# Attention scores in 17 stretches with one half-filled PSUM bank each, in place of 16 full ones

## The chip, the core and the metric

The kernel runs on one core of a Trainium2 chip. The metric is the device time of one execution in microseconds (us); lower is better. TensorE is called PE in the profile, its weight loads PEld; VectorE is DVE, ScalarE is ACT, GpSimd is POOL, SyncE is SP.

## The reference, cut to what matters

Three residual blocks follow each other on x of 4 x 1024 x 512, each closed by a layer normalisation: an attention, a gated convolution over two taps, and a ternary feed-forward. The change touches the attention alone:

```python
q = _lin(_lin(x, wq_w, wq_b), vq_w, vq_b)      # k and v in the same way
q = q.reshape(b, s, hc, H).transpose(2, 0, 1, 3)   # 32 heads (hc) of 16 columns (H)
scores = jnp.einsum('cbqh,cbkh->cbqk', q, k) / scale
attn = jax.nn.softmax(scores, axis=-1)
o = jnp.einsum('cbqk,cbkh->cbqh', attn, v)
o = o.reshape(H, b, s, hc).transpose(1, 2, 0, 3).reshape(b, s, f)
return _lin(o, wo_w, wo_b)
```

So there are 4 batches with 32 heads each, 1024 queries and 1024 keys, and a head has 16 columns.

## The kernel before

**Units.** The attention is cut into 32 units. A unit is four heads of one batch. Each of the four heads sits in its own group of 32 partitions (two halves, high and low, of 16 columns), so that its score products use 32 rows of TensorE's array and the four heads use four different row groups.

**Two passes over the scores.** Every score is computed twice. `nat(u, ...)` (L696, product at L712) makes scores with queries on the partitions, 128 queries by 512 keys in one PSUM bank, from two products of 512 columns. DVE takes each row's largest (`mx`, L725, written negated). When half of a unit is done, two keys' halves are joined (`least`, L730), POOL splits the result in a high and a low part (`neg`, L734), and `shift` (L741) turns it (L745) and sends it through DRAM into the rows `m_rows`. `scores(u, ...)` (L761, product at L791) then makes the scores with keys on the partitions, 128 keys by 256 queries, from three products of 256 columns: two for the halves of q and k, one that adds the negated maximum (`ones` times `m_rows`). Two such blocks fill one PSUM bank. ACT takes the exponential of the whole bank into an `at` tile (L800).

**V products.** `weigh(u, i)` (L818, products at L828) multiplies the exponentials with V for 256 queries and half of the keys: 16 products, 32 instructions, on 128 rows and 32 columns for each head. The result is copied by ACT (L839, first half of the keys) or added by DVE (L841, second half) into `o_sb`.

**Pieces.** Between these blocks lie pieces of other work. `product` (L531, products through `by_quarters`, L60, named `part`) makes a part of the q and k projections of later units, in 8 calls of 256 or 512 columns; `v_products` (L612, `v`) makes one or two parts of the next batch's V; `out_products` (L657, `po`) makes parts of the output projection in the last units. ACT copies a piece out of its bank (L549 and L547, L628, L670), POOL adds it where it belongs. `fill` is the list of pieces that a unit has to issue; `out_pieces` is the list that serves the last units.

**PSUM.** Eight banks: pool `ps_st` has four, taken in turn by `scores`, and `ps_nat` has four, taken in turn by `nat`. `bank` (L597) gives a V product or a piece the next bank of `ps_nat` while `between[0]` is true, as it is in units 0 to 30, and otherwise one of `ps_st`. A bank can be filled again when DVE or ACT has read it.

**Order.** The schedule is written out by hand; each engine runs its instructions in the order in which they are issued. Unit u takes the scores of its own heads for the exponentials and, in the same stretch, the maxima of unit u + 1. A unit has 32 half steps h (`HS`). At each even h stands a *stretch*: one call of `issue` (L805) with `nat` of heads 0 and 1, `scores` of heads 2 and 3, `nat` of heads 2 and 3, `scores` of heads 0 and 1. `issue` sorts the products by the columns that their head has already been given in this stretch, so that the four row groups fill evenly; behind the products come the four reductions and the four exponentials. A stretch fills all eight banks and is followed in turn by a V product (at h % 4 == 1, for the scores that were complete one stretch earlier, through the list `weighing`) and by a piece (at h % 4 == 3). So the order on TensorE is stretch, V product, stretch, piece, and so on: 16 stretches, 8 V products and 8 pieces in a unit. Other work (the stages of `shift` and of the normalisation, loads of q and k, the sends in `due`) hangs on fixed values of h.

The setup (unit -1) and the last unit (31) have orders of their own.

Of the kernel before, what the change touches and what calls it, by code (L numbers as in the profile page):

```python
# [8 lines left out]
F32 = mybir.dt.float32  # L9
# [290 lines left out]
def attention(ctx, tc, a, attn_d, ident, shared, hand):  # L300
# [130 lines left out]
                nc.vector.tensor_copy(w_d[:, f, :], pts[f])  # L431
    units = [(b, g) for b in range(B) for g in range(NG)]
    NU = len(units)
    HS = 32

# [135 lines left out]
    def products(p, which):  # L573


        return [
            [
                lambda part=part: product(p, which, *part)
                for part in parts
            ]  # L580
            for parts in (
                [(1, 0, 256), (1, 256, 256), (6, 0, 256), (6, 256, 256), (2, 0, 256), (2, 256, 256)],
                [(7, 0, 512), (5, 0, 512), (3, 0, 256), (3, 256, 256), (4, 0, 256), (4, 256, 256)],
            )
        ]

# [95 lines left out]

    out_parts = [(0, [(1, t), (2, t)]) for t in range(4)] + [(0, [(3, t), (3, t + 1)]) for t in (0, 2)]
    out_parts += [(0, [(i, t)]) for t in range(4) for i in (6, 7, 5, 4)]
    out_parts += [(2, [(1, t), (2, t)]) for t in range(4)] + [(2, [(3, t)]) for t in range(3)]
    out_parts += [(2, [(3, 3), (6, 0)])] + [(2, [(6, t)]) for t in range(1, 4)] + [(2, [(5, t)]) for t in range(4)]
    out_pieces = [lambda part=part: out_products(*part) for part in out_parts]
    out_pieces += [lambda i=i, t=t: out_products(2, [(i, t)], i == 4 or t == 3) for i in (4, 7) for t in range(4)]  # L690

    mxs, turned, o_sbs = {}, {}, {}

    def nat(u, i, pair, apart=False):  # L696


        qt, kh = divmod(i, 2)
        if i == 0 and pair == 0:  # L700
            mxs[u] = small.tile([P, NT, 4, 2], F32, tag="mx", name=f"mx{u}")
        pool, tag = (ps_st, "st") if apart else (ps_nat, "nat")
        pts = [pool.tile([P, 512], F32, tag=tag, name=f"nat{u}_{i}_{pair}_{n}") for n in range(2)]
        works = []
        for n in range(2):
            r = 32 * (2 * pair + n)
            for turn in range(2):
                works.append(
                    (
                        2 * pair + n,  # L710
                        512,
                        lambda n=n, r=r, turn=turn: nc.tensor.matmul(  # L712
                            pts[n],
                            qk_sets[u % 3][turn][r : r + 32, qt * P : (qt + 1) * P],
                            qk_sets[u % 3][2][r : r + 32, kh * 512 : kh * 512 + 512],
                            start=turn == 0,
                            stop=turn == 1,
                        ),
                    )
                )  # L720

        def reduce():
            for n in range(2):
                j = 2 * pair + n
                nc.vector.tensor_reduce(mxs[u][:, qt, j, kh : kh + 1], pts[n], AX.X, ALU.max, negate=True)  # L725
            if i % 8 == 7 and pair == 1:
                half = i // 8
                ts = slice(4 * half, 4 * half + 4)
                least = small.tile([P, 4, 4], F32, tag="least", bufs=1, name=f"least{u}_{half}")
                nc.vector.tensor_tensor(  # L730
                    least.rearrange("p c t -> p t c"), mxs[u][:, ts, :, 0], mxs[u][:, ts, :, 1], ALU.min
                )
                parts = negs[half].rearrange("p (c a t) -> p a c t", c=4, a=2)
                nc.gpsimd.tensor_copy(parts[:, 0].bitcast(F32R), least)  # L734
                nc.gpsimd.tensor_sub(parts[:, 1], least, parts[:, 0])

        return works, reduce

    rows_d = {}

# [17 lines left out]

    ats = {}

    def scores(u, i, pair, wide=False):  # L761


        qq, kp = divmod(i, 4)
        made = []
        for n in range(2):
            j = 2 * pair + n
            if wide:
                made.append((j, ps_nat.tile([P, 512], F32, tag="nat", name=f"stw{u}_{i}_{j}")))
            else:  # L770
                made.append((j, ps_st.tile([P, 512], F32, tag="st", name=f"st{u}_{i}_{j}")))
        works = []
        cols = slice(qq * QW, qq * QW + QW)
        hl, lh, ks = qk_sets[u % 3]
        for k in range(2):
            kt = 2 * kp + k
            for j, st in made:
                r = slice(32 * j, 32 * j + 32)
                two = slice(32 * j, 32 * j + 2)
                for n, (left, right) in enumerate(  # L780
                    (
                        (ks[r, kt * P : (kt + 1) * P], hl[r, cols]),
                        (ks[r, kt * P : (kt + 1) * P], lh[r, cols]),
                        (ones[two, :], m_rows[two, cols]),
                    )
                ):
                    works.append(
                        (
                            j,
                            QW,  # L790
                            lambda st=st, k=k, n=n, left=left, right=right: nc.tensor.matmul(  # L791
                                st[:, k * QW : k * QW + QW], left, right, start=n == 0, stop=n == 2
                            ),
                        )
                    )

        def exponentials():
            for j, st in made:
                at = atp.tile([P, 512], F32, tag="at", name=f"at{u}_{i}_{j}")
                nc.scalar.activation(at, st, AF.Exp, scale=0.25)  # L800
                ats[u, i, j] = at

        return works, exponentials

    def issue(*both):  # L805

# [11 lines left out]
    def weigh(u, i):  # L818


        b, g = units[u]
        qq, half = divmod(i, 2)
        av = bank(f"av{u}_{i}", QW)
        for n in range(4):
            kt = 4 * half + n
            for j in range(4):
                c = 4 * g + j
                nc.tensor.matmul(  # L828
                    av[32 * j : 32 * j + 32, :],
                    v_sb[b % 2][:, kt, c * VW : c * VW + 32],  # L830
                    ats[u, 2 * i + n // 2, j][:, n % 2 * QW : n % 2 * QW + QW],
                    start=n == 0,
                    stop=n == 3,
                )
        if i == 0:
            o_sbs[u] = obuf.tile([P, S], F32, tag="o_sb", name=f"o_sb{u}")
        o = o_sbs[u][:, qq * QW : qq * QW + QW]
        if half == 0:
            nc.scalar.copy(o, av)  # L839
        else:  # L840
            nc.vector.tensor_add(o, av, o)  # L841
        if i == 7:
            stages.extend([lambda k=k: normalise(u, k) for k in range(4)])
# [69 lines left out]
    for u in range(-1, NU):  # L913
# [4 lines left out]
        if p < NU // 2:  # L918
            if w % 2 == 0:
                parts = products(p, w // 2)  # L920
                if p == 14 and w == 0:


                    parts[0].pop()
                    parts[0].append(lambda: product(14, 0, 2, 256, 128))
                    parts[1].insert(0, lambda: product(14, 0, 2, 384, 128))
            fill += parts[w % 2]
        if u == -1:
            def sums():
# [6 lines left out]
            ] + fill  # L936
        elif units[u][0] + 1 < B:
            b, g = units[u][0] + 1, units[u][1]
            v1, v2 = (lambda n=n, b=b: v_products(b, v_parts[n]) for n in (2 * g, 2 * g + 1))

            fill = {
                0: fill[:2] + [v1] + fill[2:4] + [v2] + fill[4:],
                1: [v1, v2] + fill,
                2: fill[:2] + [v1] + fill[2:4] + [v2] + fill[4:],
                3: fill + [v1, v2],
            }[w]
        if w == 2 and p + 2 < NU // 2:
            due.setdefault((u, 24), []).append(lambda p=p: sum_w(p + 2, 0))
# [16 lines left out]
        if u == -1:  # L965
            total, done, steps = len(fill), 0, HS // 3 + 1
            for n in range(steps):
                hs = range(3 * n, min(3 * n + 3, HS))
                issue(*[nat(0, h // 2, h % 2, apart=h % 2 == 1) for h in hs])
                if n in (0, 1):  # L970
                    load_qk(1, n)
                if 2 <= n < 6:
# [7 lines left out]
        elif u + 1 == NU:  # L980
# [1 line left out]

            rooms[:] = [v_sums[3][:, n, :] for n in range(2)]
            for i in range(HS // 2):
                issue(scores(u, i, i % 2), scores(u, i, 1 - i % 2, wide=True))
                if i % 2 == 0 and weighing:
                    weigh(*weighing.pop(0))
                if i % 2 == 1:
                    weighing.append((u, i // 2))

                for n in range({2: 3, 4: 0, 6: 0, 14: 0}.get(i, 1 - i % 2)):
                    out_pieces.pop(0)()
                if i in (12, 14):
                    for t in (0, 4):
# [14 lines left out]
                if i in (2, 5, 8, 11) and stages:  # L1009
                    stages.pop(0)()  # L1010
        else:
            for h in range(HS):
                now = (u, h)
                if h % 2 == 0:
                    i = h // 2
                    issue(nat(u + 1, i, 0), scores(u, i, 1), nat(u + 1, i, 1), scores(u, i, 0))
                if h % 4 == 1 and weighing:
                    weigh(*weighing.pop(0))
                if h in (4, 5, 7):
                    shift(u, 1, (4, 5, 7).index(h))  # L1020
                if h in (20, 21, 23):
# [7 lines left out]
                if u + 2 < NU:  # L1029
# [2 lines left out]
                        load_qk(u + 2, 0)  # L1032
                    if h == (24 if first else 2):
                        load_qk(u + 2, 1)
                if h % 4 == 3:
                    weighing.append((u, h // 4))
                    if fill:
                        fill.pop(0)()
                    elif u > 24 or u == 24 and h > 24:
# [408 lines left out]
```

## Time and profile before

| | us |
|---|---|
| median of 3 runs (lowest, highest) | 2181.19 (2178.62, 2182.13) |
| the profiled execution | 2175.67 |
| its span, first to last instruction | 2173.5 |

| engine | busy us | share of the span | instructions |
|---|---|---|---|
| PE | 2131.1 | 98% | 33644 |
| PEld | 1522.8 | 70% | 33644 |
| DVE | 1724.9 | 79% | 3064 |
| ACT | 1389.7 | 64% | 2761 |
| POOL | 952.0 | 44% | 1123 |

The granted TensorE clock was 0.997 of full speed over the span. Busy time of PE is the union of its products' times; products overlap in the array, and a product that waits in the middle of others leaves no hole in it. So a busy PE is not a PE at its peak, and what a stretch costs is better read from the starts of its products. A wait is put down to the engine that ended it last. In the views, `<-` separates what is written from what is read, `x2` is the number of instructions that a row merges, and a bracket holds the idle time of the engine ahead of the row and what ended it.

### The profile page before, as it was taken

How to read it: one execution, taken by the hardware profiler on the slowest of the kernel's cores; microseconds unless marked ns; L12 is line 12 of the kernel's file. 1: busy time of each engine (PE TensorE's matmuls, PEld its weight loads, DVE VectorE, ACT ScalarE, POOL GpSimd, SP SyncE). 2: the span in 40 equal slices, each digit the busy share in tenths (PEclk: the TensorE clock that was granted, in tenths of full speed). 3: DMA queues.
4: the chain of work that ended last, by engine and by line, in shares of the span. 5: the costliest groups of instructions: out<-in, count | busy, mean ns of one | idle time of the engine just before them, and what ended most of it. 6: DMA issues, size and time to landing. Idle time of an engine off the chain costs nothing.

```text
span 2173.5 us, 78274 instructions
## 1 busy us (share of the span) xinstructions
PE 2131.1 (98%) x33644; PEld 1522.8 (70%) x33644; DVE 1724.9 (79%) x3064; ACT 1389.7 (64%) x2761; POOL 952.0 (44%) x1123
## 2 busy tenths in 40 slices
PE   9999999999999999999999999999999999999998
PEld 6666666666666666666666666666666699947997
DVE  3678888888888888888888888888888477779667
ACT  1157777777777777777777777777777733521336
POOL 2562443333344423333533323545364379532773
PEclk9999999999999999999999999999999999999999
DMA  7522212342312233223313123522311243270222
GB/s 270 178 61 88 72 53 86 107 124 63 101 53 73 67 101 101 63 84 90 104 57 96 54 82 114 161 62 82 114 53 36 76 160 117 73 276 20 93 83 78
DMA packets 115099, 208.00 MB, mean 96 GB/s; under 512 B 37440, under 2 KB 37696, under 8 KB 114624
## 3 DMA queue, kind: packets, MB, share of 16 engines
q1 hardware_dynamic: 114032, 201.82, 29.0%
q8 instruction: 264, 4.33, 0.8%
q10 hardware_dynamic: 720, 1.18, 0.2%
q14 instruction: 83, 0.68, 0.1%
HBM read 132.68 MB, written 69.73 MB: 93 GB/s over the span
## 4 chain that ended last, share of the span: by engine, by line
PE 84%; DVE 12%; issue 1%; POOL 1%; ACT 1%; DMA 0%; SPq 0%; DVEq 0%; ACTq 0%; POOLq 0%
PE av L828 22%; PE nat L712 17%; PE st L791 10%; PE part L60 9%; DVE mx L725 8%; PE pa L1158 6%; PE pc L1158 6%; PE v L60 4%; PE po L60 3%; PE po L291 2%; PE proj L60 1%; PE fold L424 1%; PE pf L1251 1%; PE fold L60 1%; DVE y L1256 1%
## 5 line engine op out<-in xcount | busy, mean ns | idle before, releaser
L725 DVE TENSOR_REDUCE mx<-nat 128x1 f32<-128x512 f32 x2048 | 1270.0, 682 | 222.3 <-PE nat L712 201.9
L800 ACT ACTIVATE at<-st 128x512 f32<-128x512 f32 x2016 | 1042.1, 604 | 317.7 <-PE st L791 313.0
L712 PE MATMUL nat<-qk 32*128 32x512 f32 x4096 | 742.2, 422 | 1.6 <-DVE v_sb L639 0.9
L791 PE MATMUL st<-qk 32*128 32x256 f32 x8064 | 682.8, 292 | 0.2
L791 PEld LDWEIGHTS st<-qk 32*128 32x128 f32 x8064 | 532.1, 184 | 4.7 <-issue 2.5
L712 PEld LDWEIGHTS nat<-qk 32*128 32x128 f32 x4096 | 356.6, 184 | 230.2 <-DVE mx L725 183.1
L791 PE MATMUL st<-qk,ones 2*128 2x256 f32 x4032 | 505.1, 288 | 0.0
L828 PE MATMUL av<-at,v_sb 128*32 128x256 f32 x8192 | 500.3, 383 | 2.8 <-DVE mx L725 1.4
L828 PEld LDWEIGHTS av<-at,v_sb 128*32 128x32 f32 x8192 | 241.0, 110 | 174.9 <-ACT at L800 7.4
L791 PEld LDWEIGHTS st<-qk,ones 2*128 2x128 f32 x4032 | 355.1, 183 | 0.0
L1169 ACT ACTIVATE u<-u,b_c 128x512 f32<-128x512 f32 x64 | 46.2, 722 | 159.9 <-DVE u L1168 159.9
L734 POOL CAST neg<-least 128x16 fp32r<-128x16 f32 x64 | 12.6, 196 | 249.8 <-DVE least L730 249.6
L841 DVE TENSOR_TENSOR o_sb<-av,o_sb 128x256 f32<-128x256 f32 x128 | 54.3, 424 | 68.5 <-PE av L828 68.1
L681 POOL TENSOR_TENSOR y<-y,extra 128x256 f32<-128x256 f32 x96 | 65.3, 710 | 64.2 <-ACT extra L670 64.2
L1165 DVE SCALAR_TENSOR_TENSOR u<-pa,u 128x342 f32<-128x342 f32 x64 | 40.6, 634 | 64.3 <-PE pa L1158 62.5
L644 POOL TENSOR_TENSOR v_sb<-v_sb,rooms 128x256 f32<-128x256 f32 x56 | 36.9, 688 | 122.5 <-ACT rooms L628 122.5
L877 POOL TENSOR_TENSOR o_n<-o_sb,o_n 128x512 f32<-128x512 f32 x64 | 82.4, 1309 | 13.7 <-DMA o_n<-rec_d 13.3
L449 POOL TENSOR_TENSOR extra<-extra,highs 128x512 f32<-128x512 f32 x62 | 79.4, 1280 | 5.0
L1158 PE MATMUL pa<-xf,w 128*128 128x171 f32 x512 | 80.4, 308 | 0.2 <-POOL w L195 0.2
L1158 PE MATMUL pc<-xf,w 128*128 128x171 f32 x512 | 79.8, 308 | 0.0
L644 POOL TENSOR_TENSOR v_sb<-v_sb,extra 128x256 f32<-128x256 f32 x68 | 44.8, 687 | 78.3 <-ACT extra L628 78.3
L1158 PEld LDWEIGHTS pa<-xf,w 128*128 128x128 f32 x512 | 76.0, 189 | 0.7 <-POOL w L195 0.7
(204 smaller groups left out, 2743.1 us busy)
## 6 DMA issues: line engine op xcount, KB each, us to landing
qk<-qk_d SPq DMA_DIRECT2D x96, 512.0 KB
qk_d<-highs SPq DMA_DIRECT2D x96, 256.0 KB
qk_d<-extra SPq DMA_DIRECT2D x96, 256.0 KB
u<-in_ctx SPq DMA_DIRECT2D x16, 1024.0 KB
xT<-in_xT SPq DMA_DIRECT2D x16, 512.0 KB
o_n<-rec_d SPq DMA_DIRECT2D x128, 64.0 KB
attn<-o_n SPq DMA_DIRECT2D x256, 32.0 KB
w<-in_conv_wT SPq DMA_DIRECT2D x16, 512.0 KB
```

What stands on the lines that cost most here:

```text
L60: nc.tensor.matmul(pt[r, :], lhsT(f)[:, r], rhs(f), start=f == 0, stop=f == tiles - 1)
L449: eng.tensor_sub(block, block, high)
L644: add(c, c, x)
L681: eng.tensor_add(c, c, x)
L712: lambda n=n, r=r, turn=turn: nc.tensor.matmul(pts[n], qk_sets[u % 3][turn][r : r + 32, qt * P : (qt + 1) * P], qk_sets[u % 3][2][r : r + ...
L725: nc.vector.tensor_reduce(mxs[u][:, qt, j, kh : kh + 1], pts[n], AX.X, ALU.max, negate=True)
L791: lambda st=st, k=k, n=n, left=left, right=right: nc.tensor.matmul(st[:, k * QW : k * QW + QW], left, right, start=n == 0, stop=n == 2),
L800: nc.scalar.activation(at, st, AF.Exp, scale=0.25)
L828: nc.tensor.matmul(av[32 * j : 32 * j + 32, :], v_sb[b % 2][:, kt, c * VW : c * VW + 32], ats[u, 2 * i + n // 2, j][:, n % 2 * QW : n % 2 ...
L841: nc.vector.tensor_add(o, av, o)
L877: nc.gpsimd.tensor_mul(part, o_sb[:, cols].rearrange("p (s e) -> p e s", e=2), part)
L1158: nc.tensor.matmul(pt, w[i][:, tap, o : o + P], xf[:, tap, i, :], start=i == 0, stop=i == FT - 1)
```

## The change

Units 0 to 30 have 17 stretches (`NS = 17`, so 34 half steps) in place of 16. Stretch 0 fills eight banks as before. In each later stretch one bank is filled by half, 256 of 512 columns: in the odd stretches a bank of `nat`, in the even ones a bank of `scores`. The short bank belongs to one head (`first`), which changes every two stretches in the order 0, 1, 2, 3, 0, 1, 2, 3, and its products come first in the stretch: odd stretches begin with `nat`, even ones with `scores`, of that head and its neighbour (`mine`), beside the other kind of the other two heads. The total of columns in a unit stays as it is. Counters (`asked`, `scored`) hold how far each head has come, in halves of a bank; where `nat` of a head stands at an odd count, its full bank takes four products of 256 columns in place of two of 512, since the two halves of the bank are then not one run of keys.

`between[0]` is set after every stretch: behind stretch 0 and the odd stretches the next block takes a bank of `ps_nat`, behind the even ones a bank of `ps_st`. Pieces stand behind stretch 0 and the odd stretches (h == 1 and h % 4 == 3), nine in a unit, and V products behind the even stretches from 2 on (h % 4 == 1, h > 1), eight in a unit. V product i now stands behind stretch 2i + 2 of its own unit, the last one behind stretch 16 (before, it stood in the next unit). Since a head with short banks behind it lags by one or two halves, a V product can need exponentials of the stretch right ahead of it.

To fill nine places, one of the two V pieces is cut in two in half of the units, and the 512-column `product` number 7 is cut in two in the others; some of the output's double pieces are cut as well, and the last unit starts with one piece more.

The maxima of a unit go to one tile `mx` with 32 entries for each head, one for each 256 keys of a query tile, and `largest` reduces them by half units, behind stretches 8 and 16.

```diff
-    HS = 32
+    HS, NS = 32, 17
...
-                [(7, 0, 512), (5, 0, 512), (3, 0, 256), (3, 256, 256), (4, 0, 256), (4, 256, 256)],
+                [(7, 0, 256), (7, 256, 256), (5, 0, 512), (3, 0, 256), (3, 256, 256), (4, 0, 256), (4, 256, 256)],
...
+    def nat(u, banks, apart=False):
+        made, works = [], []
+        for j, s, n in banks:
+            pool, tag = (ps_st, "st") if apart else (ps_nat, "nat")
+            pt = pool.tile([P, 512], F32, tag=tag, name=f"nat{u}_{j}_{s}")
+            made.append((j, s, n, pt))
+            r = slice(32 * j, 32 * j + 32)
+            whole = n == 2 and s % 2 == 0
+            for m in range(1 if whole else n):
+                qt, kq = divmod(s + m, 4)
+                cols = 512 if whole else QW
...
         def reduce():
+            for j, s, n, pt in made:
+                x = pt[:, 0 : n * QW].rearrange("p (n c) -> p n c", n=n)
+                nc.vector.tensor_reduce(mx[:, j, s : s + n], x, AX.X, ALU.max, negate=True)
...
+    def largest(u, half):
+        least = small.tile([P, 4, 4], F32, tag="least", bufs=1, name=f"least{u}_{half}")
+        each = mx[:, :, 16 * half : 16 * half + 16].rearrange("p c (t k) -> p c t k", k=4)
+        nc.vector.tensor_reduce(least, each, AX.X, ALU.min)
...
         def exponentials():
+            for j, s, n, st in made:
+                at = atp.tile([P, 512], F32, tag="at", name=f"at{u}_{j}_{s}")
+                nc.scalar.activation(at[:, 0 : n * QW], st[:, 0 : n * QW], AF.Exp, scale=0.25)
+                for m in range(n):
+                    ats[u, j, s + m] = at[:, m * QW : m * QW + QW]
...
+    def stretch(u, n):
+        if n == 0:
+            asked[:] = [0] * 4
+            scored[:] = [0] * 4
+        turn = (n - 1) // 2
+        first = turn % 4 if n else 0
+        mine, others = (first, first ^ 1), (2 - 2 * (first // 2), 3 - 2 * (first // 2))
+        def banks(at, heads, short):
+            made = []
+            for j in heads:
+                count = 1 if short and j == first else 2
+                made.append((j, at[j], count))
+                at[j] += count
+            return made
+        fewer_scores = n > 0 and n % 2 == 0
+        fewer_nat = n % 2 == 1
+        if fewer_scores:
+            issue(
+                scores(u, banks(scored, mine, True)),
+                nat(u + 1, banks(asked, others, False)),
+                scores(u, banks(scored, others, False)),
+                nat(u + 1, banks(asked, mine, False)),
+            )
+        else:
+            issue(
+                nat(u + 1, banks(asked, mine, fewer_nat)),
+                scores(u, banks(scored, others, False)),
+                nat(u + 1, banks(asked, others, False)),
+                scores(u, banks(scored, mine, False)),
+            )
+        if n in (NS // 2, NS - 1):
+            largest(u + 1, n // (NS - 1))
+        between[0] = not fewer_scores
...
-            v1, v2 = (lambda n=n, b=b: v_products(b, v_parts[n]) for n in (2 * g, 2 * g + 1))
+            v1, v2 = v_parts[2 * g : 2 * g + 2]
+            v2 = [[part] for part in v2] if w % 2 == 0 else [v2]
+            v1, *v2 = [lambda part=part, b=b: v_products(b, part) for part in [v1] + v2]
...
-            for h in range(HS):
+            for h in range(2 * NS):
                 now = (u, h)
                 if h % 2 == 0:
-                    i = h // 2
-                    issue(nat(u + 1, i, 0), scores(u, i, 1), nat(u + 1, i, 1), scores(u, i, 0))
-                if h % 4 == 1 and weighing:
-                    weigh(*weighing.pop(0))
+                    stretch(u, h // 2)
+                if h % 4 == 1 and h > 1:
+                    weigh(u, h // 4 - 1)
...
-                if h % 4 == 3:
-                    weighing.append((u, h // 4))
+                if h % 4 == 3 or h == 1:
                     if fill:
                         fill.pop(0)()
```

More of the change, by code (lines that the diff above doesn't have):

```diff
@@ L681, in out_products @@
                     eng.tensor_add(c, c, x)
-    out_parts = [(0, [(1, t), (2, t)]) for t in range(4)] + [(0, [(3, t), (3, t + 1)]) for t in (0, 2)]
+    out_parts = [(0, [(i, t)]) for t in range(4) for i in (1, 2)] + [(0, [(3, t)]) for t in range(4)]
     out_parts += [(0, [(i, t)]) for t in range(4) for i in (6, 7, 5, 4)]
-    out_parts += [(2, [(1, t), (2, t)]) for t in range(4)] + [(2, [(3, t)]) for t in range(3)]
+    out_parts += [(2, [(1, 0)]), (2, [(2, 0)])] + [(2, [(1, t), (2, t)]) for t in range(1, 4)]
+    out_parts += [(2, [(3, t)]) for t in range(3)]
     out_parts += [(2, [(3, 3), (6, 0)])] + [(2, [(6, t)]) for t in range(1, 4)] + [(2, [(5, t)]) for t in range(4)]
@@ L690, in attention @@
     out_pieces += [lambda i=i, t=t: out_products(2, [(i, t)], i == 4 or t == 3) for i in (4, 7) for t in range(4)]
[L694 to L718, printed above, removed]
+    turned, o_sbs = {}, {}
@@ new lines, in attention @@
+    mx = small.tile([P, 4, HS], F32, tag="mx", bufs=1, name="mx")
+    def nat(u, banks, apart=False):
[9 more added lines that the diff above has]
+                cols = 512 if whole else QW
+                for turn in range(2):
+                    works.append(
+                        (
+                            j,
+                            cols,
+                            lambda pt=pt, m=m, r=r, qt=qt, kq=kq, cols=cols, turn=turn: nc.tensor.matmul(
+                                pt[:, m * QW : m * QW + cols],
+                                qk_sets[u % 3][turn][r, qt * P : (qt + 1) * P],
+                                qk_sets[u % 3][2][r, kq * QW : kq * QW + cols],
+                                start=turn == 0,
+                                stop=turn == 1,
+                            ),
+                        )
@@ L719, in nat @@
                     )
-                )
         def reduce():
[L723 to L735, printed above, removed]
@@ L737, in nat @@
-        return works, reduce
+            for j, s, n, pt in made:
+                x = pt[:, 0 : n * QW].rearrange("p (n c) -> p n c", n=n)
+                nc.vector.tensor_reduce(mx[:, j, s : s + n], x, AX.X, ALU.max, negate=True)
+        return works, reduce
+    def largest(u, half):
+        least = small.tile([P, 4, 4], F32, tag="least", bufs=1, name=f"least{u}_{half}")
+        each = mx[:, :, 16 * half : 16 * half + 16].rearrange("p c (t k) -> p c t k", k=4)
+        nc.vector.tensor_reduce(least, each, AX.X, ALU.min)
+        parts = negs[half].rearrange("p (c a t) -> p a c t", c=4, a=2)
+        nc.gpsimd.tensor_copy(parts[:, 0].bitcast(F32R), least)
+        nc.gpsimd.tensor_sub(parts[:, 1], least, parts[:, 0])
@@ L759, in attention, with scores @@
     ats = {}
[L761 to L773, printed above, removed]
-        hl, lh, ks = qk_sets[u % 3]
[L775 to L780, printed above, removed]
+    def scores(u, banks, wide=False):
+        made, works = [], []
+        hl, lh, ks = qk_sets[u % 3]
+        for j, s, n in banks:
+            pool, tag = (ps_nat, "nat") if wide else (ps_st, "st")
+            st = pool.tile([P, 512], F32, tag=tag, name=f"st{u}_{j}_{s}")
+            made.append((j, s, n, st))
+            r = slice(32 * j, 32 * j + 32)
+            two = slice(32 * j, 32 * j + 2)
+            for m in range(n):
+                qq, kt = divmod(s + m, NT)
+                cols = slice(qq * QW, qq * QW + QW)
+                for k, (left, right) in enumerate(
                     (
@@ L790, in scores @@
                             QW,
-                            lambda st=st, k=k, n=n, left=left, right=right: nc.tensor.matmul(
-                                st[:, k * QW : k * QW + QW], left, right, start=n == 0, stop=n == 2
+                            lambda st=st, m=m, k=k, left=left, right=right: nc.tensor.matmul(
+                                st[:, m * QW : m * QW + QW], left, right, start=k == 0, stop=k == 2
                             ),
@@ L797, in exponentials @@
         def exponentials():
[L798 to L801, printed above, removed]
-        return works, exponentials
+            for j, s, n, st in made:
+                at = atp.tile([P, 512], F32, tag="at", name=f"at{u}_{j}_{s}")
+                nc.scalar.activation(at[:, 0 : n * QW], st[:, 0 : n * QW], AF.Exp, scale=0.25)
+                for m in range(n):
+                    ats[u, j, s + m] = at[:, m * QW : m * QW + QW]
+        return works, exponentials
+    def stretch(u, n):
[27 more added lines that the diff above has]
+                scores(u, banks(scored, mine, False)),
+            )
+        if n in (NS // 2, NS - 1):
+            largest(u + 1, n // (NS - 1))
+        between[0] = not fewer_scores
+    asked, scored = [0] * 4, [0] * 4
     def issue(*both):
@@ L830, in weigh @@
                     v_sb[b % 2][:, kt, c * VW : c * VW + 32],
-                    ats[u, 2 * i + n // 2, j][:, n % 2 * QW : n % 2 * QW + QW],
+                    ats[u, j, NT * qq + kt],
                     start=n == 0,
@@ L920, in attention @@
                 parts = products(p, w // 2)
-                if p == 14 and w == 0:
+                if u > 0 and units[u][1] == NG - 1:
                     parts[0].pop()
-                    parts[0].append(lambda: product(14, 0, 2, 256, 128))
-                    parts[1].insert(0, lambda: product(14, 0, 2, 384, 128))
+                    parts[0] += [lambda t=t, p=p: product(p, 0, 2, t, 128) for t in (256, 384)]
             fill += parts[w % 2]
@@ L938, in attention @@
             b, g = units[u][0] + 1, units[u][1]
-            v1, v2 = (lambda n=n, b=b: v_products(b, v_parts[n]) for n in (2 * g, 2 * g + 1))
+            v1, v2 = v_parts[2 * g : 2 * g + 2]
+            v2 = [[part] for part in v2] if w % 2 == 0 else [v2]
+            v1, *v2 = [lambda part=part, b=b: v_products(b, part) for part in [v1] + v2]
             fill = {
[L942 to L945, printed above, removed]
+                0: fill[:2] + [v1] + fill[2:4] + v2 + fill[4:],
+                1: [v1] + v2 + fill,
+                2: fill[:2] + [v1] + fill[2:4] + v2 + fill[4:],
+                3: fill + [v1] + v2,
             }[w]
@@ L968, in attention @@
                 hs = range(3 * n, min(3 * n + 3, HS))
-                issue(*[nat(0, h // 2, h % 2, apart=h % 2 == 1) for h in hs])
+                issue(
+                    *[
+                        nat(0, [(2 * (h % 2) + n, h // 2 * 2, 2) for n in range(2)], apart=h % 2 == 1) for h in hs
+                    ]
+                )
+                for half in range(2):
+                    if 16 * half + 15 in hs:
+                        largest(0, half)
                 if n in (0, 1):
@@ L984, in attention @@
             for i in range(HS // 2):
-                issue(scores(u, i, i % 2), scores(u, i, 1 - i % 2, wide=True))
+                pairs = [[(2 * pair + n, 2 * i, 2) for n in range(2)] for pair in (i % 2, 1 - i % 2)]
+                issue(scores(u, pairs[0]), scores(u, pairs[1], wide=True))
                 if i % 2 == 0 and weighing:
@@ L989, in attention @@
                     weighing.append((u, i // 2))
-                for n in range({2: 3, 4: 0, 6: 0, 14: 0}.get(i, 1 - i % 2)):
+                for n in range({0: 2, 2: 3, 4: 0, 6: 0, 14: 0}.get(i, 1 - i % 2)):
                     out_pieces.pop(0)()
```

## The prediction, made before the changed kernel ran

> **What bounds the kernel now.** I read the page's chain of waits first, then the busy times of single attention units, then one stretch pair in order of time. A "block" is a run of TensorE work of one kind; its length is from its first product to the next block's first.
>
> ```profile
> PE 84%; DVE 12%; issue 1%; POOL 1%; ACT 1%; DMA 0%; SPq 0%; DVEq 0%; ACTq 0%; POOLq 0%
> PE av L828 22%; PE nat L712 17%; PE st L791 10%; PE part L60 9%; DVE mx L725 8%; PE pa L1158 6%; PE pc L1158 6%; PE v L60 4%; PE po L60 3%; PE po L291 2%; PE proj L60 1%; PE fold L424 1%; PE pf L1251 1%; PE fold L60 1%; DVE y L1256 1%
> ```
>
> TensorE's order sets the time; the row maxima (`mx`) are the one other thing of weight on it. By stretch (columns: window, us, busy of PE, PEld, DVE, ACT, POOL):
>
> ```profile
> 880.10:928.40 48.30, 47.76 (x901) 32.79 (x897) 42.15 (x74) 36.91 (x78) 11.65 (x18) 1.00 0.20 58
> 1080.60:1130.40 49.80, 49.33 (x932) 33.85 (x928) 41.32 (x72) 37.33 (x78) 19.14 (x25) 1.00 0.16 46
> 1130.40:1181.50 51.10, 50.72 (x932) 33.28 (x928) 42.16 (x74) 38.14 (x79) 21.02 (x27) 1.00 0.28 89
> ```
>
> Each is one unit of 16 stretches, 8 V products and 8 pieces. The first has short pieces alone (256 columns, 16 instructions), the second has two long ones (two products, or 512 columns), the third four. So a short pair of stretches with its piece and V product takes 48.3/8 = 6.04 us, and a long piece adds (49.8 - 48.3)/2 = 0.75 or (51.1 - 48.3)/4 = 0.70. DVE and ACT have 6 to 11 us of room in a unit: neither bounds it as a whole, only at places. One short pair in order of time (start, us, engine, line):
>
> ```profile
> 809.18 0.50 PE L712 MATMUL nat<-qk 32*128 32x512 f32 x2
> 809.18 0.50 PE L791 MATMUL st<-qk 32*128 32x256 f32 x4
> ...
> 809.52 0.28 PE L791 MATMUL st<-qk,ones 2*128 2x256 f32 x2
> ...
> 809.88 0.38 PE L791 MATMUL st<-qk,ones 2*128 2x256 f32 x4
> ...
> 809.94 3.80 DVE L725 TENSOR_REDUCE mx<-nat 128x1 f32<-128x512 f32 x6
> ...
> 810.25 2.07 ACT L800 ACTIVATE at<-st 128x512 f32<-128x512 f32 x4 [1.24 <-PE st L791]
> 810.34 0.28 PE L791 MATMUL st<-qk,ones 2*128 2x256 f32 x2
> 810.69 0.59 PEld L60 LDWEIGHTS part<-x_sums,w_sums 128*32 128x32 f32 x16 [0.27 <-DVE mx L725]
> ...
> 811.69 0.68 PE L712 MATMUL nat<-qk 32*128 32x512 f32 x2
> ...
> 811.89 0.38 PE L791 MATMUL st<-qk 32*128 32x256 f32 x2
> ...
> 812.18 0.41 ACT L549 COPY extra<-part 128x256 f32<-128x256 f32 x1
> ...
> 812.71 0.42 PE L712 MATMUL nat<-qk 32*128 32x512 f32 x2
> ...
> 813.11 0.28 PE L791 MATMUL st<-qk,ones 2*128 2x256 f32 x2
> 813.31 0.14 PEld L828 LDWEIGHTS av<-at,v_sb 128*32 128x32 f32 x6
> ```
>
> Three readings. **One:** the four heads run side by side. At 809.18 `nat` of two heads and `st` of the other two start together, and a head's three score products of 256 columns take 0.36 us (809.52 to 809.88), 0.12 each. A head has 2 x 512 `nat` and 6 x 256 `st` columns, 2560 in a chain of its own; a stretch lasts as long as the longest chain, not as the sum. **Two:** the first stretch takes 1.51 us (809.18 to 810.69). Its last product starts 1.16 after its first; where nothing is waited for, the next block follows 0.20 after the last start (813.11 to 813.31). So 1.37 of the 1.51 is work and 0.14 the wait for the first `nat` bank's maximum. **Three:** the second stretch takes 1.62: 0.20 at its start, where a `nat` bank's maximum is late (811.69 to 811.89, and in-order `st` products stand behind it), the rest smaller. The V product takes 1.86, the short piece 1.00: 1.51 + 1.00 + 1.62 + 1.86 = 5.99.
>
> **The change, part by part.**
>
> *A 17th stretch.* Columns are the same, but the half bank is taken from one head only; the other three still have 2560 columns. So each stretch's floor stays 1.37, and a unit's floor grows by 1.37 us: 31 units (0 to 30) x 1.37 = 42 us, certain unless reading one is wrong.
>
> *A ninth piece* (1.00 short). No work is new: with the last V part or the 512-column product split, a unit goes from 2 long + 6 short to 1 + 8, or from 4 + 4 to 3 + 6.
>
> *The wait ahead of the piece goes.* In odd stretches the short head's `nat` half comes first. Its reduce starts about 0.55 after the stretch's start and lasts between 0.42 (the 256-wide add, L841) and 0.68 (today's), so it ends by 1.23 at worst, ahead of 1.37. Odd stretch: 1.38, gain 0.13.
>
> *The even stretch.* What is late next is ACT. Count from the odd stretch's start. Its four exponentials run as today, from 1.07 (810.25) to 3.14, and the piece's copy behind them from 3.00 to 3.41 (812.18 plus 0.41). Neither is shortened: odd stretches have four full score banks. The even stretch now starts at 1.38 + 1.00 = 2.38. Its first `nat` banks are free (maxima at about 1.5 and 2.1), so the 0.20 goes. But its fourth score bank is wanted at 2.38 + 0.56 = 2.94 and free at 3.14, and the last head's `nat` takes the piece's bank, free at 3.46 with some 0.05 for the semaphore. Products of all heads queue behind each such wait. From that `nat` to the next block took 0.60 today (812.71 to 813.31): 4.06. Today the V product starts at 4.13. So the even stretch is 1.68, and the pair 1.38 + 1.00 + 1.68 + 1.86 = 5.92, a gain of 0.07. Bounds for the even stretch: 1.37 (no wait) to 1.85 (the two waits add up).
>
> *The unit's start.* Stretch 0 is full and a piece follows it: 1.51 + 1.00 as today, then stretch 1 as today's second (1.62), a piece (1.00, its half bank free), stretch 2 (1.60; ACT has three stretches and two copies to serve, about 6.2 us of 6.7) and the V product (1.86): 8.59.
>
> *V products directly behind.* A V product used scores at least one stretch old. The short heads fall behind, so from the second V product on some head's last quarter, and for the last two V products two heads' last half, comes from the stretch just ahead. Its exponentials would end about 5.25 on the scale above; the third quarter of the V product starts at 4.06 + 0.93 = 4.99, the fourth at 5.42. So two V products per unit wait up to 0.26 each; queued behind are the next stretch's products. Bounds 0 to 0.5 a unit; I take 0.3, as the exponentials' 0.48 pitch is the row. Short exponentials have no row: between 0.376 (the 256-wide copy) and 0.604, before the full ones and under TensorE work either way. The Trainium skill (ScalarE: Activation LUTs, What ACT_TABLE_LOAD costs) gives 186 ns + 0.833 a column, 0.40 for it; the V bank it frees is free either way.
>
> *Split products.* Where a head's count of halves is odd, a `nat` bank takes four products of 256 for two of 512 (some 28 banks a unit). The row: 0.12 for 256 against 0.24 for 512 (812.71 to the same heads' next at 812.95), so nothing. The Trainium skill speaks against it (TensorEngine Tiling (Array Packing), Instruction Overhead): some 60 cycles per matmul. By that, two more products in a chain would cost an estimated 0.05 a stretch, about 23 us in all; the row does not show it, and I add none.
>
> *At nothing:* `largest` (two small reduces a unit for two 0.19 adds, under V products; if uncovered 0.5 a unit), moved DMA issues (the piece's sends keep their four steps, the last at the next unit's step 3 as today; `load_qk` keeps a unit of lead), the merged `mx`.
>
> **Sum.** Unit with short pieces: 8.59 + 7 x 5.92 = 50.0 against 8 x 5.99 = 47.9: +2.1. A long piece takes 1.87 and gives ACT time to catch up; I put the even stretch behind it at 1.50, near today's 1.53 there, so it adds 0.87 - 0.18 = 0.69. Units with two long pieces: +2.1 + 0.69 - 1.50 = +1.3; with four: +2.1 + 3 x 0.69 - 2.8 = +1.4. With 0.3 for the V products about 1.6, times 31 = +50 us. The profiled execution took 2175.67 us (span 2173.5), so it would be 2226; the median of the runs, 2181.19, stands 5.5 above it: 2231. Own range: even stretch 1.60 to 1.78 and V waits 0 to 0.5 give about +20 to +78, 2201 to 2259.
>
> **Rivals.**
> - *Every bank wait goes (faster, 0.10).* ACT keeps ahead and all stretches take 1.38: 17 x 1.38 + 9 + 8 x 1.86 = 47.3; with the long pieces a unit gains about 1.0, so -30 us, 2151. It decides from an even stretch under 1.50 (8 x 0.19 cancels 1.5). For: DVE's idle time. Against: four exponentials at 0.48 in a row after 1.07 cannot end before 3.
> - *Half banks do shorten the stretch (no change, 0.12).* If heads share a limit, a stretch takes 15/16, 16 x 0.09 = 1.4 a unit comes back, and +50 becomes about +7: 2188. Against: the equal starts at 809.18.
> - *V products stall in earnest (0.15).* If ACT falls further behind, five V products a unit wait 0.4: +2.0 for 0.3, 2284. For: their waits on exponentials of the same stretch. Against: ACT's room, 11 us a unit.
>
> The forecast has 0.63. The range 2184 to 2274 leaves out the first rival, part of the second and most of the third. Differences under 0.2% (4.4 us), about what a measurement of this kernel can tell from none, are most likely in the second rival: faster 0.12, same 0.05, slower 0.83.
>
> **What would show it.** Right: stretches ahead of pieces at 1.38, those ahead of V products at 1.6 to 1.75 with waits for exponentials and for the piece's copy where `mx` stood, units near 51.5 to 53 us, the share of `mx` on the chain well under 8%. Wrong: odd stretches at 1.3 or less (heads share), even ones under 1.5, or V products well over 1.86 in the middle.

## The result, and the profile after

| | before | after |
|---|---|---|
| median of 4 runs, us | 2181.66 | 2267.29 |
| lowest, highest | 2178.62, 2182.64 | 2265.72, 2270.48 |
| ratio, 95% interval | | 1.0397, 1.0379 to 1.0415 |
| profiled execution, its span | 2175.67, 2173.5 | 2270.48, 2268.7 |

The change costs 86 us. The forecast was +50 us (2231), with a range from 2184 to 2274. The profiled execution after is the slowest of its four, so sizes below are taken from its units, not from the spans.

The chain of waits after (the two lines that answer to the first fence of the prediction):

```profile
PE 91%; DVE 4%; DMA 2%; issue 1%; POOL 1%; ACT 1%; SPq 0%; DVEq 0%; ACTq 0%; POOLq 0%
PE st L788 24%; PE av L866 22%; PE nat L716 13%; PE part L60 8%; PE pa L1203 6%; PE pc L1203 6%; PE v L60 4%; PE po L60 2%; PE po L291 2%; PE fold L424 1%; DMA b_vd<-b_vc 1%; PE pf L1296 1%; DVE stats L1302 1%; DVE y L1301 1%; DMA y<-in_x 0%
```

The maxima (`mx`, 8% before) are gone from it, as intended, and `st` has risen from 10% to 24%. ACT's 1% is misleading: a stretch that waits for ACT in one head's products has other heads' products running, and the chain goes through those. The experiments below bring ACT out.

Three units after, at the same places as those of before (short pieces alone; units that had two long pieces; units that had four):

```profile
929.50:981.70 52.20, 51.40 (x983) 35.78 (x980) 42.94 (x77) 37.48 (x81) 13.09 (x20) 1.00 0.15 48
1142.50:1195.10 52.60, 52.60 (x999) 36.34 (x996) 42.92 (x77) 37.97 (x82) 18.54 (x26) 1.00 0.14 44
1195.10:1249.40 54.30, 54.19 (x1011) 36.55 (x1008) 42.83 (x77) 38.82 (x83) 21.13 (x28) 1.00 0.29 86
```

They were 48.3, 49.8 and 51.1 us: +3.9, +2.8 and +3.2. From the start of unit 0 to the end of unit 30 the traces have 1553.8 us before and 1643.3 after, with one V product more (1.86), which stood in unit 31 before: most of the loss lies there (89.5 of the 95.2 us between the two spans). DVE and ACT have the same work as before to within 1.6 us.

Where in a unit? The table gives the median length of each block over units 1 to 23, read from the starts of the products.

| | before | after |
|---|---|---|
| stretches ahead of a V product | 0, 2, ... 14: 1.54 to 1.71, mean 1.63 | 2: 1.60; 4, 6, ... 16: 1.55 to 1.67, mean 1.62 |
| stretches ahead of a piece | 1, 3, ... 15: 1.51 | 0: 1.59; 1: 1.72; 3, 5, ... 15: 1.51, 1.59, 1.47, 1.59, 1.55, 1.57, 1.46, mean 1.53 |
| sum of a unit's stretches | 25.12 | 27.01 |
| V products | 1.86 | 1.86; behind stretch 14 2.14, behind stretch 16 2.33 |
| short piece | 1.00 | 1.00 |

1.89 for the stretches, 0.74 for the two V products and 0.13 to 0.15 for the piece that is split make 2.77 a unit, times 31 units 86 us. The means over units 1 to 30 agree: 1.99, 0.76 and 0.11 us, together 2.86.

An odd and an even stretch of unit 17 after, in order of time:

```profile
1063.61 0.39 PE L716 MATMUL nat<-qk 32*128 32x256 f32 x2
...
1063.82 0.42 DVE L879 TENSOR_TENSOR o_sb<-av,o_sb 128x256 f32<-128x256 f32 x1 [0.19 <-PE av L866]
...
1064.16 2.33 DVE L729 TENSOR_REDUCE mx<-nat 128x1 f32<-128x256 f32 x4
...
1064.20 0.49 PE L788 MATMUL st<-qk 32*128 32x256 f32 x4
...
1064.52 0.28 PE L788 MATMUL st<-qk 32*128 32x256 f32 x1
...
1064.79 2.07 ACT L797 ACTIVATE at<-st 128x512 f32<-128x512 f32 x4 [1.89 <-PE st L788]
...
1065.21 1.07 PE L60 MATMUL v<-w_v,xT 128*32 128x256 f32 x16
1066.21 0.18 PEld L788 LDWEIGHTS st<-qk 32*128 32x128 f32 x2 [0.41 <-ACT at L797]
...
1066.71 0.41 ACT L628 COPY rooms<-v 128x256 f32<-128x256 f32 x1
...
1066.92 0.50 PE L716 MATMUL nat<-qk 32*128 32x512 f32 x1
...
1067.17 0.38 PE L716 MATMUL nat<-qk 32*128 32x256 f32 x1
...
1067.83 0.42 PE L866 MATMUL av<-at,v_sb 128*32 128x256 f32 x4
```

The piece at 1065.21 starts 0.21 us behind the last product (at 1065.00): its wait for a maximum is gone. But the stretch still took 1.60. DVE's add (L879) reads the V product's bank until 1064.24, and that bank is the fourth score bank of this stretch: the partner head's first score product starts at 1064.30 (merged into the row at 1064.20), 0.69 after the stretch's start instead of the 0.57 of a run without this wait (v_nat, below), and its second, with weights loaded late, at 1064.52. The four exponentials of this stretch run from 1064.79 to 1066.86. The even stretch begins at 1066.21 with banks that are free; its score product in the bank that the last exponential frees starts at 1066.91, and its `nat` product in the bank of the piece, which ACT copies until 1067.12, at 1067.17.

The V product behind stretch 16:

```profile
1086.19 2.40 PE L866 MATMUL av<-at,v_sb 128*32 128x256 f32 x32
1087.04 0.15 PEld L866 LDWEIGHTS av<-at,v_sb 128*32 128x32 f32 x2 [0.26 <-ACT at L797]
1087.53 0.58 PEld L866 LDWEIGHTS av<-at,v_sb 128*32 128x32 f32 x14 [0.34 <-ACT at L797]
```

It stops twice for exponentials of the stretch right ahead of it. So it is in every unit: this V product takes 2.27 us or more in all 31.

### The profile page after: what moved, and what is told of

The parts are those of the page before. It is cut to its first block, busy times and chain, and to the rows that moved or that the text cites. A ratio compares the mean times of both kernels' runs of the same rounds, so it can differ in the third digit from the quotient of the medians.

```text
span 2268.7 us, 83442 instructions
## 1 busy us (share of the span) xinstructions
PE 2239.1 (99%) x35884; PEld 1608.2 (71%) x35884; DVE 1746.7 (77%) x3189; ACT 1407.2 (62%) x2901; POOL 954.4 (42%) x1139
## 4 chain that ended last, share of the span: by engine, by line
PE 91%; DVE 4%; DMA 2%; issue 1%; POOL 1%; ACT 1%; SPq 0%; DVEq 0%; ACTq 0%; POOLq 0%
PE st L788 24%; PE av L866 22%; PE nat L716 13%; PE part L60 8%; PE pa L1203 6%; PE pc L1203 6%; PE v L60 4%; PE po L60 2%; PE po L291 2%; PE fold L424 1%; DMA b_vd<-b_vc 1%; PE pf L1296 1%; DVE stats L1302 1%; DVE y L1301 1%; DMA y<-in_x 0%
## 5 line engine op out<-in xcount | busy, mean ns | idle before, releaser
L729 DVE TENSOR_REDUCE mx<-nat 128x2 f32<-128x512 f32 (+1 forms) x2172 | 1294.2, 653 | 280.3 <-PE nat L716 274.7
L797 ACT ACTIVATE at<-st 128x512 f32<-128x512 f32 x2172 | 1109.9, 582 | 329.3 <-PE st L788 324.7
L716 PE MATMUL nat<-qk 32*128 32x256 f32 (+1 forms) x6080 | 824.7, 344 | 7.9 <-DVE v_sb L639 3.7
L788 PE MATMUL st<-qk 32*128 32x256 f32 x8192 | 811.4, 303 | 1.0 <-DVE o_sb L879 0.5
L788 PEld LDWEIGHTS st<-qk 32*128 32x128 f32 x8192 | 654.8, 184 | 124.3 <-ACT at L797 108.4
L788 PE MATMUL st<-qk,ones 2*128 2x256 f32 x4096 | 640.1, 288 | 0.0
L716 PEld LDWEIGHTS nat<-qk 32*128 32x128 f32 x6080 | 529.8, 184 | 133.0 <-DVE mx L729 47.2
L788 PEld LDWEIGHTS st<-qk,ones 2*128 2x128 f32 x4096 | 467.4, 183 | 0.0
L866 PEld LDWEIGHTS av<-at,v_sb 128*32 128x32 f32 x8192 | 252.5, 109 | 188.6 <-ACT at L797 27.5
L877 ACT COPY o_sb<-av 128x256 f32<-128x256 f32 x128 | 48.0, 375 | 114.5 <-PE av L866 97.9
L879 DVE TENSOR_TENSOR o_sb<-av,o_sb 128x256 f32<-128x256 f32 x128 | 54.3, 424 | 69.7 <-PE av L866 68.2
L1203 PEld LDWEIGHTS pc<-xf,w 128*128 128x128 f32 x512 | 76.0, 189 | 0.0
```

Of the source, the lines that this page charges most:

```text
L716: lambda pt=pt, m=m, r=r, qt=qt, kq=kq, cols=cols, turn=turn: nc.tensor.matmul(pt[:, m * QW : m * QW + cols], qk_sets[u % 3][turn][r, qt * ...
L729: nc.vector.tensor_reduce(mx[:, j, s : s + n], x, AX.X, ALU.max, negate=True)
L788: lambda st=st, m=m, k=k, left=left, right=right: nc.tensor.matmul(st[:, m * QW : m * QW + QW], left, right, start=k == 0, stop=k == 2),
L797: nc.scalar.activation(at[:, 0 : n * QW], st[:, 0 : n * QW], AF.Exp, scale=0.25)
L866: nc.tensor.matmul(av[32 * j : 32 * j + 32, :], v_sb[b % 2][:, kt, c * VW : c * VW + 32], ats[u, j, NT * qq + kt], start=n == 0, stop=n == 3,)
L1203: nc.tensor.matmul(pt, w[i][:, tap, o : o + P], xf[:, tap, i, :], start=i == 0, stop=i == FT - 1)
```

## The experiments

**v_nat: the V product's bank back in the other pool.**

```diff
-        between[0] = not fewer_scores
+        between[0] = True
```

> The changed kernel with the V products' bank taken from the nat pool after every stretch, as in the kernel before. Theory one: the odd stretches' 1.46 to 1.59 us (against a floor of 1.38) come from the fourth score bank, which the V product holds until ACT or DVE has read it; with the bank in the other pool odd stretches fall to 1.38 to 1.42, after ACT's copies and DVE's adds alike, some 1.2 us a unit over 31 units: about 2230 us. Rival: the excess is the price of the split nat products (34 to 38 products a stretch) and of more switches; then odd stretches stay at 1.46 to 1.59 and the time at 2267 within 8 us.

Measured: 2253.88 us (2252.49 to 2255.85), ratio to the kernel before 1.0342 (1.0323 to 1.0361). The odd stretches fell to 1.39 to 1.40, all seven alike, with 32, 34, 36 or 38 products and behind ACT's copies and DVE's adds. That settles their excess: it was the V product's bank, and neither the split products nor switching costs more than the 0.01 between them. But of the 37 us that were expected only 13 came. The even stretches rose from a mean of 1.62 to 1.71: odd and even together went from 3.16 to 3.10. What the odd stretch gives, the even one takes back.

```profile
1064.59 0.39 PE L716 MATMUL nat<-qk 32*128 32x256 f32 x2
...
1065.67 2.07 ACT L797 ACTIVATE at<-st 128x512 f32<-128x512 f32 x4 [1.72 <-PE st L788]
...
1065.98 1.07 PE L60 MATMUL part<-xT,w_qk 128*32 128x256 f32 x16
1066.98 0.18 PEld L788 LDWEIGHTS st<-qk 32*128 32x128 f32 x2 [0.41 <-ACT at L797]
1067.59 0.41 ACT L549 COPY extra<-part 128x256 f32<-128x256 f32 x1
...
1067.79 0.18 PEld L788 LDWEIGHTS st<-qk 32*128 32x128 f32 x1 [0.16 <-ACT at L797]
...
1068.05 0.38 PE L716 MATMUL nat<-qk 32*128 32x256 f32 x1
...
1068.72 0.42 PE L866 MATMUL av<-at,v_sb 128*32 128x256 f32 x4
```

From the odd stretch's start: exponentials from 1.08 to 3.15, the copy to 3.41, a score product that waited for the last exponential at 3.20, a `nat` product in the piece's bank at 3.46 (0.05 behind the copy; other products were running, so its row shows no idle time), the V product at 4.13. In the pair of the kernel before that the prediction shows, the V product stood at 4.13 as well. Over all pairs with a short piece in units 1 to 23, the median from the odd stretch's start to the V product is 4.14 before, 4.21 after and 4.13 in v_nat.

**v_old: V products without the wait for fresh exponentials.** The index into the exponentials is capped at what was complete one stretch earlier (`prior`, a copy of `scored` made at the head of `stretch`):

```diff
+        prior[:] = scored
...
-                    ats[u, j, NT * qq + kt],
+                    ats[u, j, min(NT * qq + kt, prior[j] - 1) if u + 1 < NU else NT * qq + kt],
...
+            nc.vector.tensor_scalar_max(recs[u], recs[u], 1e-30)
```

So this kernel leaves the freshest exponentials out of its result, and older ones stand there twice.

> The changed kernel, but a V product reads, where its own exponentials come from the stretch right ahead of it, those of an older stretch in their place (other data, so part of the result is replaced; the row sums are kept above zero by one small DVE operation a unit). Theory one: the V products behind stretches 14 and 16 wait for exponentials, 0.27 and 0.47 us; they return to 1.86, and 0.74 x 31 = 23 us go: about 2244 us. Rival: ACT is late in any case and the wait reappears in the stretch or the piece that follows; then less than 8 us go.

Measured: 2238.6 us (2237.02 to 2240.06), 1.0269 (1.0253 to 1.0285). All V products take 1.86, and 29 us are gone, 0.93 a unit: the 0.74 itself and some that the stall had passed on (stretch 1 fell from 1.72 to 1.67, stretch 16 from 1.67 to 1.60). Some stretches grew by up to 0.05, but a unit's stretches together fell by 0.14, so the wait did not come back elsewhere.

**v_nat_old: both.**

> Both edits together. Theory one: the gains add up, 37 + 23 us, about 2207 us, and the rest over the kernel before (26 us) is the 17th stretch, whose 1.38 us a unit no order of banks takes away: not below 2190 us. Rival: the waits alone made the change slow and the short bank does shorten a stretch; then it falls below the kernel before, under 2181 us.

Measured: 2227.9 us (2226.93 to 2228.49), 1.022 (1.0204 to 1.0235). 39 us of the 60, about what the two edits gave one by one (13 and 29), so the 2207 was missed for the same reason as in v_nat. The rival falls: the time stays far above that of the kernel before. What is left over the kernel before is 47 us: a unit's stretches sum to 26.48 us against 25.12, and 1.36 plus 0.15 for the split piece, times 31, is 47. Odd and even average 1.39 and 1.69, together 3.08 against 3.14, so the 16 old stretches are worth hardly less than before, and the seventeenth comes on top. The even stretches still wait for ACT here (1.69, where the odd ones take 1.39), as they did before.

**together: all four heads short in the same stretches.** V products in the nat pool, and

```diff
-                count = 1 if short and j == first else 2
+                count = 1 if short else 2
...
-        fewer_scores = n > 0 and n % 2 == 0
-        fewer_nat = n % 2 == 1
+        fewer_scores, fewer_nat = n in (2, 16), n in (1, 9)
```

with `fewer_nat` and `fewer_scores` passed for `others` too, and the order within a stretch still by n's parity.

> V products in the nat pool, and the short banks of all four heads in the same stretches: nat in stretches 1 and 9, scores in 2 and 16, the other thirteen full. The columns of a unit are the same. Theory one (a stretch lasts as long as its longest head): stretch 9 has 2048 columns in every head and falls to about 1.15 us, where with one short head it takes 1.38; stretch 16 falls by up to 0.35, the V stalls shrink since no head lags by more than one half, and the pieces behind the full odd stretches wait 0.13 again: about 2200 us. Rival (the heads share a limit, so that columns in sum decide): stretch 9 no shorter than 1.30, and about 2235 us.

Measured: 2306.01 us (2303.17 to 2308.86), 1.0578 (1.056 to 1.0597). On what it was made to tell, stretch 9 gives the answer: it took 1.16 (median).

```profile
1083.79 0.38 PE L716 MATMUL nat<-qk 32*128 32x256 f32 x2
...
1084.73 0.29 PE L716 MATMUL nat<-qk 32*128 32x256 f32 x2
1084.95 0.64 PE L60 MATMUL v<-w_v,xT 128*32 128x256 f32 x8
```

The same columns left out in one head alone (v_nat, stretch 9) left it at 1.40. Where nothing else is waited for, a stretch is as long as its longest head. The other stretches that are short in all heads do not show it: 1 took 1.51, 2 took 1.96, and 16 took 1.61 and not up to 0.35 less. Other waits stand in them: in unit 17, for example, stretch 2 stood for the copy of the piece ahead of it (row below), and stretch 16 waited 0.30 us for a maximum.

```profile
1061.33 0.38 PE L716 MATMUL nat<-qk 32*128 32x256 f32 x1 [0.55 <-ACT extra L547]
```

As a forecast of time the expectation failed by 106 us: six V products, behind stretches 4 to 14, took 2.20 to 2.29, and the V products' weight loads stood idle 61 us for exponentials, against 27.5 in the changed kernel. The likely reason, read off the order and not tested: now every head's last quarter was fresh and its even stretch had four full exponentials; I had counted the halves that lag and not when the last exponential ends. And the 0.23 us that stretch 9 gained were taken back whole by stretch 10 (1.97).

**extra_one: 512 columns more in one head, in the kernel before.**

```diff
+                    if n == 0 and u + 1 < NU and j == 0:
+                        works.append(
+                            (
+                                j,
+                                QW,
+                                lambda st=st, k=k, left=left, right=right: nc.tensor.matmul(
+                                    st[:, k * QW : k * QW + QW], left, right, start=True, stop=True
+                                ),
+                            )
+                        )
```

> The kernel before (16 stretches), with the first score product of head 0 made twice in units 0 to 30: 512 columns more in one head's chain in every stretch, nothing more in the other three, the same result. Theory one (a stretch lasts as long as its longest head): 0.24 us more in a chain; ahead of a piece 0.14 of it hides in the wait for the maximum, ahead of a V product none: 0.34 a pair, 8 x 31 pairs, 84 us: about 2265 us. Rival (heads share a limit): two more products of 32, 0.08 a stretch, half of it hidden: at most 20 us, 2200 us.

Measured: 2246.58 us (2245.41 to 2247.75), 1.0303 (1.0273 to 1.0333): +66 us, three times the 20 that shared columns allow, if short of the 84 expected. Stretches ahead of a piece went from 1.51 to 1.61, the 0.10 expected; those ahead of a V product by 0.10 to 0.22, in the mean 0.15 and not 0.24, probably as part of theirs was waiting already.

**act_more and act_more_16: one exponential made twice in each stretch ahead of a piece.** In v_nat, and in the kernel before:

```diff
+            n = now[1] // 2
+            if u + 1 < NU and n % 2 and j == ((n - 1) // 2 % 4) ^ 1:
+                nc.scalar.activation(at, st, AF.Exp, scale=0.25)
```

```diff
+            if u + 1 < NU and i % 2 and j == 1:
+                nc.scalar.activation(at, st, AF.Exp, scale=0.25)
```

> The run with the V products in the nat pool, and in odd stretches the last of the four exponentials made twice (same result): ACT has 0.48 us more ahead of the release of the fourth score bank and of the piece's copy. ACT stands idle for 10 us of a unit and has 4 us more to do. Theory one (the even stretch is pinned by ACT's chain, which starts at 1.07 and runs four exponentials and a copy): even stretches behind a short piece go from 1.73 to about 2.1, some 0.4 x 7 x 31 = 87 us: about 2340 us. Rival (even stretches are pinned by the maxima on DVE or by TensorE's own order): ACT's idle time takes it up and the time stays within 10 us of 2254.

> The kernel before, with the same doubling: the last exponential of each stretch ahead of a piece is made twice. Theory one: there too ACT pins the stretch behind the piece, since it ended at the same 4.1 us after the pair's start; stretches behind short pieces go from 1.62 to about 2.0, those behind long ones hardly change: 5 to 6 of 8 pairs, 0.4 x 5.5 x 31 = 68 us, about 2250 us. Rival: before, the second stretch waited for the maxima (0.20 at its start) and not for ACT; then under 20 us.

Measured: 2375.08 us (2374.54 to 2375.62), 1.0893 (1.0861 to 1.0924), so 121 us over v_nat; and 2279.4 us (2276.98 to 2281.82), 1.0454 (1.0419 to 1.0489), 99 us over the kernel before. In act_more even stretches behind short pieces went from 1.73 to 2.30, in act_more_16 from 1.63 to 2.19 (stretches 0, 10, 12 and 14). That is about 0.57, where 0.4 was expected, and so both times lie above the forecasts. I had taken 0.48 us of ACT for the repeat; in the trace below it ends 3.72 us after the odd stretch's start, where the last exponential of v_nat ended at 3.15. ACT was later by 0.57, and the even stretch longer by as much. The page's chain of act_more, then of act_more_16:

```profile
PE 69%; ACT 23%; DVE 4%; issue 1%; POOL 1%; DMA 0%; SPq 0%; DVEq 0%; ACTq 0%; POOLq 0%
```

```profile
PE 69%; ACT 21%; DVE 6%; issue 1%; POOL 1%; DMA 1%; SPq 0%; DVEq 0%; ACTq 0%; POOLq 0%
```

And how act_more's even stretch waited, from the odd stretch's start at 1064.62:

```profile
1067.74 0.60 ACT L802 ACTIVATE at<-st 128x512 f32<-128x512 f32 x1
...
1068.39 0.38 PE L788 MATMUL st<-qk 32*128 32x256 f32 x1 [0.44 <-ACT at L802]
...
1069.32 0.42 PE L869 MATMUL av<-at,v_sb 128*32 128x256 f32 x4
```

The score product follows the repeated exponential's end by 0.05 us and the V product stands at 4.70 instead of 4.13, which is also the median over the short pairs of units 1 to 23. So ACT had no room left at this place in either kernel, though it is busy for 37 of a unit's 52 us after, and for 37 of 48 before: it stands idle until the first score banks of a stretch are full, and then has four exponentials and a copy in a row.

No run beat the kernel before, and none pointed to an order that would: 16 stretches with the pair ending at ACT's 3.4 us are what it has already.

## Why the prediction was right, and where it was off

Direction and range held; the size was short, +50 for +86. That the range held is in part luck: the one worked out from the terms ended at 2259, and 2267 lies only in the wider one. The terms also erred in both directions: odd stretches came out 0.15 longer than forecast, even ones 0.06 shorter.

- **The floor of a stretch, and the 17th.** Right. That one short head saves nothing is shown by stretch 9 of together against that of v_nat, and by extra_one. The price of the 17th stretch, 42 us, is not measured alone, but fits v_nat_old: 47 us remain without the waits for the V product's bank and in the V products, some 4 to 5 of them for the split piece.
- **The wait ahead of the piece goes; odd stretch 1.38.** The wait went, the length was wrong: 1.53 on average. The step that failed is the bank of the V product. The prediction called it free "either way" when it asked whether the V product would wait for it, and did not ask who waits for the V product to be read: the fourth score bank is wanted 0.57 us into the stretch, and the add ends at 0.63. In the kernel before, the V product's bank was in the nat pool and wanted at 0.82 (row `810.00 0.39 PE L712 MATMUL nat<-qk 32*128 32x512 f32 x2`, in the stretch that starts at 809.18). Odd stretches and stretch 0 together: 1.1 us a unit too little. v_nat gives 1.39 without it.
- **The even stretch, 1.68, pinned by ACT.** Measured 1.62 behind the longer odd stretches and, where these ran at their floor, 1.73 behind short pieces (v_nat). The mechanism, ACT's chain, is shown by the two act runs. Its last wait is where the prediction had it: `nat` in the piece's bank at 3.46. From there to the V product it took 0.67 and not 0.60. The pair, 5.92 by the sum, came to 1.39 + 1.00 + 1.73 + 1.86 = 5.98 in v_nat, against 5.99: the gain ahead of the piece is worth nothing here.
- **Stretch 1, 1.62.** Measured 1.72, and 1.67 without the V stalls.
- **V products directly behind.** Right mechanism, right places (the last two), mis-sized, and by its effect the term that missed most (see the sum): 0.3 a unit taken, 0.74 measured, 0.93 with what it passed on (v_old), above the bound of 0.5. I counted one wait for each; the third quarter of the V product behind stretch 16 waited twice, for two heads whose exponentials come one after the other (0.26 and 0.34 us of idle weight loads). The short exponentials, put at 0.40, took 0.43 in the mean of 248.
- **Split products at nothing.** Right: 1.39 with 32 products and 1.40 with 38 (v_nat). The 60 cycles a product that the Trainium skill gives (TensorEngine Tiling (Array Packing), Instruction Overhead) would have been an estimated 0.05 us a stretch, and these stretches differ by 0.01.
- **The sum.** Stretches +1.1 in the forecast and +1.89 measured, V products +0.3 and +0.74, the split piece +0.13 in both: 1.2 us a unit too little, 37 us in all by these rounded terms, about the 36 between 50 and 86. By the experiments, v_old's 29 us are some 20 more than the 0.3 a unit that was taken, and the bank is worth 13 (v_nat): 33 of the 36.
- **The rivals.** That every wait goes is refuted by ACT's chain; that short banks shorten the stretch, by extra_one and by stretch 9 of together against that of v_nat. The third, V products that stall in earnest, was nearest: 0.74 against the 2.0 of its price.

## What to carry to other kernels

Where row groups of the array run side by side, as here, work taken from one of them saves nothing; take it from all or leave it. A wait that is removed ahead of a block counts only if the next engine in line was not due at the same moment behind it, so find the point where two chains meet again (here the V product, 4.13 us after the pair's start) and ask what sets that. When a buffer moves to another pool, ask first who takes it next and how early, and only then whether its own writer waits.

## What was not expected of the hardware

A product whose weight load has waited is followed by its next product 0.22 us later and not 0.12 (1064.30 to 1064.52 after, and again 1068.39 to 1068.61 in act_more), so a start that was 0.12 us late cost this stretch 0.21 (1.60 against 1.39). And six products more in a stretch, for the same columns, made it hardly longer (1.40 against 1.39 in v_nat), though each brings a weight load of 0.18 us.
